# A graph layer with 40 instead of 32 hot regions: 640 hot slots and 1656 edges a later part

## The chip, the cores and the metric

The kernel runs on one core of a Trainium2 chip. Its time is the device time of one execution in microseconds (us), and less is better. A core has five engines that run their own instruction streams: PE (matmuls; PEld is its weight load), DVE, ACT, POOL and SP. Semaphores order them; DMA queues are fed by SP (plain transfers) and POOL (indirect gathers).

## The reference, cut to what matters

```python
def ref(x, src, dst, W1, b1, W2, b2, W4, b4):
    theta = x[dst] - x[src]
    w = sigmoid(relu(theta @ W1 + b1) @ W2 + b2)
    agg = segment_sum(w * theta, dst, num_segments=N)
    indeg = segment_sum(ones((E, 1)), dst, num_segments=N)
    return layernorm(x + agg + indeg * (x @ W4 + b4))
```

N = 12500 nodes of 128 values, E = 412,500 edges: 200,000 random pairs in both directions and one loop per node, sorted by dst. So the dst of consecutive edges lie close together, and their src are spread over all nodes.

## The kernel before, in words

*Edges to parts.* The edges are cut, in their sorted order, into parts. The first PLAIN = 26 parts are *early* and have 1024 edges each. After them come NF = 253 full *later* parts of CE = 1524 edges and one tail. Two parts make a block `b`, whose sums over dst cover WB = 112 nodes. `early_part(s)` and `part(s)` issue the work of step s; from the first later part on, the order in which an engine gets its instructions is the order in which the program issues them.

*Early: a table.* The first stage turns x into a table z in HBM, in twelve chunks (`table_chunk`): a row holds the node's product with W1 and the node itself. Row buffers `zbuf[4:7]` are lent to it as staging. While it runs, the early parts follow; later parts gather rows of 1 KB from z.

*Cold and hot edges.* Every edge of a later part needs two rows, that of its dst and that of its src. The dst rows come from one-hot products, since a block has few dst. Of the src rows, 1024 are *cold*: `gather(s)` brings them by eight indirect DMAs on POOL (L377) of 128 rows each, with a memset as a pause before each (L371), into one of NZ = 7 row buffers; gather(s+3) is issued in step s and waits for the last matmul of the step before (`paced`, `newest`). The rest have a src below 8192, which is in HR = 32 *hot regions* of HOT = 256 nodes, whose rows stay in SBUF (`tabs`). Each region gives a part HS = 16 slots, so a part has HK = 512 hot slots, in HQ = 4 *hot tiles* of 128.

*The hot path.* Four regions make a group; a *fetch* computes one group's hot rows for eight parts at a time. `LEADS` says how far ahead of its parts each of the eight groups is due, so that before the change there is one fetch a step. A fetch `f` goes through four functions: `hot_load` (SP, L949: the slot numbers, broadcast to all partitions), `hot_tiles` (ACT, L960 and L962: a one-hot matrix from them), `hot_products` (PE, L974: one-hot times the region's rows into the PSUM tile pd), and `hot_out` (ACT, L988: pd into xT, a ring of HX = 10 parts, in one or two writes).

*A later step.* `part(s)` runs, in this order: `hot_load` of the fetch due 7 steps later, `hot_out` of the fetch of the step before, `hot_tiles` of the one due 4 steps later (`fetch_step`), `one_hot` of a block ahead (ACT, L835 and L836), `logits` (DVE, L890, L892, L893: dst minus src rows, times w2 behind the relu, and the row sums), `gather(s+3)`, `add_part(s-1)` (PE, L1061: the weighted rows times one-hots into the PSUM tile pa), `hot_products`, `open_gate` (ACT, L897), `hot_logits` (DVE, L1032: one instruction per hot tile, from px), the sigmoid of these (ACT, L1035), `weigh` (DVE, L922: half of the cold rows), `hot_weights` (ACT, L1041: one scaling per hot tile; DVE, L1044: the one-hots owh of the hot edges), `gate_sums`, `one_hot_w` (DVE, L871: the one-hots ow of the cold edges), `weigh_rest` (ACT, L913: four scalings), and `products_ahead(s+1, s+2)` (PE: px of the next part by transposes of xT in L1013, by W1 in L1016 and the dst rows in L1020, and y of the part after it in L1024). Every second step ends a block: `total` (ACT, L1099), `finish` (DVE, L1107), `own` (ACT, L1115 and L1116), `shift`, `normalize`. Last comes `spend`, for the placement.

*Placement.* Parts are placed in sets of 64 (`place`): set 0 in the early stage, set i from part 26 + 64 i - 72 on (set 1 from the first later parts). Its edges lie as lists on 128 partitions, WL = 763 elements each. A set runs one *round* per hot region: a MAX8 (L548) finds the next eight edges of the region in each list, a MATCH_REPLACE8 (L551) takes them out, and one operation (L544) prepares the next region. Then a scan of the cold edges in NC = 5 chunks, and the results go to HBM (`hot_s`, `rows_d`). All this is a generator of steps, nearly all on DVE. `spend` lets `part(s)` run steps as long as it has *credit*: a part brings 3.0, a "k" step costs 0.85, an "s" step 3.5, an "m" step 2.5. `load(i)` (L181 and on) reads a set's edges; in the last set some of the 64 rows are missing and are filled with constants.

*The bank of constants.* The PSUM tile `fix` is one bank of 512 floats a partition: iota_f (112), own_f (128, written by `own`), w2_b (128) and gate (16). L871 and L1044 read iota_f, L892 reads w2_b, L897 writes gate and L922 reads it. px has a tile of two banks: hot_y in one, hot_x in the other, four tiles of 128 columns each, so that both are full.

*Fallback.* Every part checks that its edges found a slot and its block's dst fit the 112 nodes. If any did not, a flag sends the program to `any_dst`, which computes everything again, from the edges as they come.

## Time and profile before

| | |
|---|---|
| time, median of 3 runs | 3644.98 us (3637.49 to 3654.82) |
| the profiled execution | 3640.54 us, of which the span of its instructions 3638.8 |
| mean granted TensorE clock | 0.866 of full speed |
| gathers (L377) | 2028, 968 ns each in the mean |
| fetches' slot numbers (L949) | 226 transfers of 128 KB |

A line of the profile's table of groups gives a source line, engine and operation, output and inputs, the count, then the busy time with the mean in ns, and the idle time just before such instructions with what ended it. A row of the timeline gives the start and the duration in us, then engine, line and operation, and in brackets the wait before it with its releaser; "x4" is four like instructions in a row, with the time from the first's start to the last's end. A row of windows gives the window, its length, busy us and count for each engine asked for, then the granted clock, the share of DMA time and GB/s.

The early stage takes the first 479 us; part 26, the first later one, follows. The placements of sets 1 to 3 begin in steps 29, 85 and 149, three steps behind their loads.

### The profile page before, as it was taken

To read this page: it belongs to the slowest core of one execution; us is meant where nothing else is said; L and a number is where in the kernel's file an instruction comes from. 1 tells how busy PE (TensorE), PEld (TensorE's weight loads), DVE (VectorE), ACT (ScalarE), POOL (GpSimd) and SP (SyncE) were. 2 spreads that over 40 slices of the span, in tenths; PEclk is the share of its full clock that TensorE was granted. 3 is DMA by queue.
4 is the path that set the end of the run, shared out by engine and by line. 5 is a ranking of instruction groups with operands and counts; after the bars stand their busy time and mean duration, and the time that the engine had idled before them with its cause. 6 is when DMAs were issued, how large, how long until landed. Compare 5 with 4: busy or idle time off the path is not lost.

```text
span 3638.8 us, 60470 instructions
## 1 busy us (share of the span) xinstructions
PE 2670.6 (73%) x17515; PEld 2263.0 (62%) x17515; DVE 2627.9 (72%) x6043; ACT 2325.4 (64%) x5830; POOL 2940.3 (81%) x4273
## 2 busy tenths in 40 slices
PE   6797877766777776777676677666777777777776
PEld 5575666666666666666665566656666666666665
DVE  7365448888886789888765788989765565666556
ACT  5364667666666766666765666665766666666664
POOL 5436378888888888888888788888888888888884
PEclk9587878888889889888898788988888999899987
DMA  8333244444444444444443344444444444444442
GB/s 261 126 100 95 72 119 110 117 118 113 120 115 125 118 118 120 111 120 116 117 121 110 103 116 119 117 114 119 117 115 119 120 117 117 119 119 113 120 113 64
DMA packets 272672, 425.92 MB, mean 117 GB/s; under 512 B 67255, under 2 KB 181466, under 8 KB 272334
## 3 DMA queue, kind: packets, MB, share of 16 engines
q0 software_dynamic: 106304, 289.03, 28.7%
q1 hardware_dynamic: 164060, 126.53, 12.7%
q10 hardware_dynamic: 1970, 6.40, 0.6%
q8 instruction: 146, 2.39, 0.3%
q14 instruction: 192, 1.57, 0.1%
HBM read 393.72 MB, written 28.01 MB: 116 GB/s over the span
## 4 chain that ended last, share of the span: by engine, by line
DVE 30%; ACT 19%; PE 19%; issue 10%; POOL 9%; another core or an unknown queue 8%; DMA 2%; SPq 1%; DVEq 0%; POOLq 0%; ACTq 0%
POOL zbuf L377 6%; DVE zbuf L892 4%; DVE zbuf L890 4%; DVE lg L893 4%; PE pa L1061 4%; DVE hh L1032 3%; ACT wxh L1041 3%; ACT zbuf L913 3%; ACT of L960 3%; POOL rest_t L371 2%; PE px L1016 2%; PE px L1020 2%; PE pd L974 2%; ACT oh L835 2%
## 5 line engine op out<-in xcount | busy, mean ns | idle before, releaser
L377 POOL DMA_INDIRECT zbuf<-z,src_i x2028 | 1963.3, 968 | 454.1 <-issue 310.1
L371 POOL MEMSET rest_t<- 128x320 f32 x2028 | 774.0, 382 | 1.0
L974 PE MATMUL pd<-of,tabs 128*128 128x128 f32 (+3 forms) x4176 | 587.7, 296 | 162.3 <-ACT of L962 79.2
L974 PEld LDWEIGHTS pd<-of,tabs 128*128 128x128 f32 x4176 | 541.6, 208 | 198.7 <-issue 99.8
L1013 PE MATMUL px<-wni,xT 128*128 128x128 f32 x1016 | 207.7, 338 | 612.4 <-ACT wxh L1041 492.9
L1061 PE MATMUL pa<-zbuf,ow 128*112 128x260 f32 (+1 forms) x2444 | 627.6, 398 | 24.1 <-issue 14.8
L1013 PEld LDWEIGHTS px<-wni,xT 128*128 128x128 f32 x1016 | 133.3, 166 | 662.0 <-ACT wxh L1041 527.2
L1032 DVE SCALAR_TENSOR_TENSOR hh<-px,w_r 128x128 f32<-128x128 f32 x1016 | 294.1, 289 | 343.5 <-remote 277.6
L1061 PEld LDWEIGHTS pa<-zbuf,ow 128*112 128x112 f32 x2444 | 418.6, 192 | 160.0 <-issue 58.2
L1024 PE MATMUL y<-y,oh 64*128 64x128 f32 x2032 | 399.7, 341 | 12.2 <-issue 10.9
L1020 PE MATMUL px<-y,oh 64*128 64x128 f32 x2032 | 391.7, 340 | 12.4 <-issue 11.5
L913 ACT ACTIVATE zbuf<-zbuf 128x128 f32<-128x128 f32 x1224 | 389.0, 390 | 0.4
L988 ACT ACTIVATE xT<-pd 128x512 f32<-128x512 f32 (+7 forms) x436 | 169.8, 411 | 340.8 <-remote 181.4
L1016 PE MATMUL px<-wni,xT 128*128 128x128 f32 x2032 | 371.9, 342 | 5.4 <-issue 5.3
L1020 PEld LDWEIGHTS px<-y,oh 64*128 64x128 f32 x2032 | 324.6, 236 | 62.1 <-issue 47.1
L1016 PEld LDWEIGHTS px<-wni,xT 128*128 128x128 f32 x2032 | 343.8, 254 | 8.9 <-issue 8.8
L960 ACT ACTIVATE of<-hot_src,nodes 128x512 f32<-128x512 f16 (+2 forms) x522 | 340.5, 702 | 12.1 <-PE pd L974 7.8
L1024 PEld LDWEIGHTS y<-y,oh 64*128 64x128 f32 x2032 | 326.4, 236 | 21.1 <-issue 20.5
L892 DVE SCALAR_TENSOR_TENSOR zbuf<-zbuf,fix 128x1024 f32<-128x1024 f32 x254 | 310.1, 1221 | 17.5
L890 DVE TENSOR_TENSOR zbuf<-y,zbuf 128x1024 f32<-128x1024 f32 x254 | 309.9, 1220 | 15.2 <-PE y L1024 3.6
L893 DVE TENSOR_REDUCE lg<-zbuf 128x8 f32<-128x1024 f32 x254 | 309.8, 1220 | 8.7
L1061 PE MATMUL pa<-wxh,owh 128*112 128x130 f32 x2032 | 292.6, 279 | 21.5 <-issue 20.0
(286 smaller groups left out, 4376.1 us busy)
## 6 DMA issues: line engine op xcount, KB each, us to landing
to_all<-off_d SPq DMA_DIRECT2D x254, 128.0 KB
zbuf<-z,src_i POOLq DMA_INDIRECT x2028
hot_src<-hot_s SPq DMA_DIRECT2D x226, 128.0 KB
z<-zbuf SPq DMA_DIRECT2D x12, 1024.0 KB
xw<-in_x_dram SPq DMA_DIRECT2D x140, 56.0 KB
u<-u_d SPq DMA_DIRECT2D x140, 56.0 KB
out_dram<-o SPq DMA_DIRECT2D x140, 56.0 KB
y<-z SPq DMA_DIRECT2D x272, 28.0 KB
```

What stands on the lines that cost most here:

```text
L371: rest = nc.gpsimd.memset(rest_t, 0.0) if s >= PLAIN else nc.gpsimd.engine_nop()
L377: ins = nc.gpsimd.indirect_dma_start(out=rows_of(s)[:, k, :], out_offset=None, in_=z if s >= NH else x, in_offset=IndirectOffsetOnAxis(ap= ...
L890: nc.vector.tensor_sub(half, yy.to_broadcast([P, 2, J, D]), half)
L892: nc.vector.scalar_tensor_tensor(h, h, 0.0, w2.to_broadcast([P, K, D]), op0=OP.max, op1=OP.mult)
L893: nc.vector.tensor_reduce(lg[:, :, 0], h, AX.X, OP.add)
L913: nc.scalar.activation(wx[:, k, :D], wx[:, k, :D], AF.Copy, scale=wx[:, k, D:D + 1])
L960: nc.scalar.activation(of[:, t, :], hot_src[:, i % NU, :w], AF.Abs, bias=nodes[:, t:t + 1])
L974: newest[0] = nc.tensor.matmul(to[:, q], tabs[:, g * RG + q, t, :], of[:, t, q], start=t == 0, stop=t == HT - 1)
L1016: nc.tensor.matmul(hot_y(s, q), xT[:, q * P:(q + 1) * P], wneg, start=q == 0, stop=False, skip_group_check=True)
L1020: newest[0] = nc.tensor.matmul(hot_y(s, q), parts[s]["oh"][:, BP + q * P:BP + (q + 1) * P], y_of(s), start=False, stop=True, skip_group_ch ...
L1024: newest[0] = nc.tensor.matmul(y[:, q, :], parts[t]["oh"][:, q * P:(q + 1) * P], y_of(t), start=True, stop=True)
L1061: newest[0] = nc.tensor.matmul(to if len(w.shape) == 3 else to[:, 0, :], one, w, start=first and i == 0, stop=last and i == len(terms) - 1)
```

## The change

HR goes from 32 to 40: the hot regions now cover src below 10240, a part has 640 hot slots in five hot tiles, and CE rises from 1524 to 1656. The cold slots stay 1024, so gathers and cold work per part stay as they are. There are 233 full later parts and a tail where there were 253 and a tail, lists of 829 elements for 763, and 40 rounds for 32 in a placement; the scan has four chunks for five.

px's two banks have no room for a fifth hot tile. Its hot_y and hot_x go to `fix` (`last_y`, `last_x`); own_f moves to SBUF for it. products_ahead, hot_logits and hot_weights loop over HQ as before, now five times.

Ten fetches come in eight steps, so two of eight steps get two. `fetch_step` goes: a step builds the tiles of its first fetch as before and does its products right after `add_part`, with a lead of 3 for 4 steps; the second fetch's hot_out of the first and its own hot_tiles stand on ACT between `one_hot_w` and `weigh_rest`, its products on PE after `products_ahead`. `hot_load` is issued 5 instead of 7 steps ahead. NZ goes from 7 to 6. The table chunks take two lent row buffers and a piece of xT in place of three row buffers. The transposes of hrel in the placement go in groups of four and one.

```diff
-NZ = 7
+NZ = 6
+LEAD = 3
...
-HR = 32
+HR = 40
-LEADS = (0, 1, 2, 3, 4, 5, 6, 7)
+LEADS = (0, 1, 2, 2, 3, 4, 5, 6, 6, 7)
-CE = 1524
+CE = 1656
...
     fix = cps.tile([P, 512], F32, name="fix")
     iota_f = fix[:, :WB].rearrange("p (o m) -> p o m", o=1)
-    own_f = fix[:, WB:WB + D]
-    w2_b = fix[:, WB + D:WB + 2 * D]
+    w2_b = fix[:, WB:WB + D]
+    last_y = fix[:, 2 * P - 2 * K:3 * P - 2 * K]
+    last_x = fix[:, 3 * P - 2 * K:4 * P - 2 * K]
+    assert WB + D <= 2 * P - 2 * K and HQ == G + 1
+    own_f = const.tile([P, D], F32, name="own_f")
     gate = fix[:, 512 - 2 * K:].rearrange("p (i k) -> p i k", k=K)
     w2_f = w2_r.rearrange("p (o m) -> p o m", o=1)
...
+    stage = [t[:, :, :2 * D] for t in zbuf[NX:]]
+    stage.append(xT_flat[:, HX * HK - 2 * BE:].rearrange("p (k d) -> p k d", k=K))
+    assert late_at + 2 * NS <= HX * HK - 2 * BE
...
         hrel = pp.tile([P, S2, HQ], BF16, name="hrel")
-        pt = scratch()[:, :HQ * P].rearrange("p (q j) -> p q j", q=HQ)
-        for q in range(HQ):
...
+        for q0 in range(0, HQ, G):
+            n_q = min(G, HQ - q0)
+            pt = scratch()[:, :n_q * P].rearrange("p (q j) -> p q j", q=n_q)
...
-        NC = 5
+        NC = 4
...
-            zt = zbuf[NX + c % 3][:, :, :2 * D]
+            zt = stage[c % len(stage)]
...
         def hot_y(s, q):
-            return parts[s]["px"][:, q * P:(q + 1) * P]
+            return parts[s]["px"][:, q * P:(q + 1) * P] if q < G else last_y
 
         def hot_x(s, q):
-            return parts[s]["px"][:, P * G + q * P:P * G + (q + 1) * P]
+            return parts[s]["px"][:, P * G + q * P:P * G + (q + 1) * P] if q < G else last_x
...
                 for q in range(HQ):
-                    nc.tensor.matmul(hot_x(s, q), xT[:, q * P:(q + 1) * P], ident, start=q == 0,
+                    nc.tensor.matmul(hot_x(s, q), xT[:, q * P:(q + 1) * P], ident, start=q % G == 0,
                                      stop=False, is_transpose=True, skip_group_check=True)
                 for q in range(HQ):
-                    nc.tensor.matmul(hot_y(s, q), xT[:, q * P:(q + 1) * P], wneg, start=q == 0,
+                    nc.tensor.matmul(hot_y(s, q), xT[:, q * P:(q + 1) * P], wneg, start=q % G == 0,
                                      stop=False, skip_group_check=True)
...
-        def fetch_step(s):
-
-            for f in rest_of:
-                if f[0] - 4 == s:
-                    hot_tiles(f)
-                    tiled.append(f)
+        def due_at(s, lead):
+            return [f for f in rest_of if f[0] - lead == s]
...
-            for f in due + [f for f in rest_of if max(f[0] - 7, PLAIN - 3) == s]:
+            for f in due + [f for f in rest_of if max(f[0] - 5, PLAIN - 3) == s]:
                 hot_load(f)
...
+            now = due_at(s, 3)
+            for f in now[:-1]:
+                hot_tiles(f)
+                hot_out(f, hot_products(f))
+            for f in now[-1:]:
+                hot_tiles(f)
+                if s == PLAIN - 1:
+                    opened.append((f, hot_products(f)))
+                else:
+                    tiled.append(f)
             if s + 2 >= PLAIN:
                 one_hot(PLAIN + 2 * h)
...
             for f in rest_of:
-                if f[0] - 7 == s:
+                if f[0] - 5 == s:
                     hot_load(f)
...
             if opened:
                 hot_out(*opened.pop())
             advance("c")
-            fetch_step(s)
+            now = due_at(s, 3)
+            if now:
+                hot_tiles(now[0])
             if h == 1 and s + 3 < NS:
                 one_hot(s + 3)
             if s < NS:
                 logits(s)
-            if PLAIN + AHEAD <= s + 3 < NS:
+            if PLAIN + AHEAD <= s + LEAD < NS:
                 if s >= PLAIN + 4:
-                    paced[s + 3] = newest[0]
-                gather(s + 3)
+                    paced[s + LEAD] = newest[0]
+                gather(s + LEAD)
             if PLAIN <= s - 1 < NS:
                 add_part(s - 1)
-            if tiled:
-                f = tiled.pop()
-                opened.append((f, hot_products(f)))
+            if now:
+                opened.append((now[0], hot_products(now[0])))
             if s < NS:
                 open_gate(s)
                 hot_logits(s)
...
                 hot_weights(s)
                 gate_sums(s)
                 one_hot_w(s)
+                if now[1:]:
+                    hot_out(*opened.pop())
+                    hot_tiles(now[1])
                 weigh_rest(s)
                 products_ahead(s + 1, s + 2)
+                if now[1:]:
+                    opened.append((now[1], hot_products(now[1])))
```

More of the change, by code (lines that the diff above doesn't have):

```diff
@@ L574, in place @@
         hrel = pp.tile([P, S2, HQ], BF16, name="hrel")
-        pt = scratch()[:, :HQ * P].rearrange("p (q j) -> p q j", q=HQ)
-        for q in range(HQ):
-            nc.tensor.matmul(pt[:, q, :], hd[:, q * P:(q + 1) * P], ident_b, start=True, stop=True)
-        if i:
-            yield "c"
-        for at in (slice(h * S2, (h + 1) * S2) for h in range(LISTS)):
-            nc.scalar.activation(hrel[at].rearrange("p j q -> p q j"), pt[at, :, at], AF.Copy)
+        for q0 in range(0, HQ, G):
+            n_q = min(G, HQ - q0)
+            pt = scratch()[:, :n_q * P].rearrange("p (q j) -> p q j", q=n_q)
+            for q in range(n_q):
+                nc.tensor.matmul(pt[:, q, :], hd[:, (q0 + q) * P:(q0 + q + 1) * P], ident_b,
+                                 start=True, stop=True)
+            if i:
+                yield "c"
+            for at in (slice(h * S2, (h + 1) * S2) for h in range(LISTS)):
+                nc.scalar.activation(hrel[at, :, q0:q0 + n_q].rearrange("p j q -> p q j"), pt[at, :, at],
+                                     AF.Copy)
         hot_s = dram.tile([HR // RG, S2, LISTS, RG * HE], F16, name=f"hot_s{i}")
```

9 lines of the change are left out of this document (3 added, 6 removed).

## The prediction

> **What bounds the kernel now.** I read the page first: its span, its busy line and its forty slices.
>
> ```profile
> span 3638.8 us, 60470 instructions
> ...
> PE 2670.6 (73%) x17515; PEld 2263.0 (62%) x17515; DVE 2627.9 (72%) x6043; ACT 2325.4 (64%) x5830; POOL 2940.3 (81%) x4273
> ...
> DVE  7365448888886789888765788989765565666556
> ...
> POOL 5436378888888888888888788888888888888884
> ```
>
> POOL sits at 8 tenths from slice 7 to the last but one, whatever the others do. DVE alternates: three plateaus of 8 to 9 and stretches of 5 to 6. The plateaus are the placements of sets 1 to 3 (`place`), the rest is plain part work. So I counted parts (one L893 each) by stage; the columns are DVE time in L893 and its count, then clock, DMA share, GB/s.
>
> ```profile
> 1262.00:1580.00 318.00, 31.72 (x26) 0.87 0.42 116
> 902.00:997.00 95.00, 8.54 (x7) 0.86 0.43 119
> 997.00:1097.00 100.00, 10.98 (x9) 0.89 0.43 117
> 2700.00:3450.00 750.00, 74.42 (x61) 0.91 0.43 118
> ```
>
> A part takes 318/26 = 12.2 us during the 32 rounds of a placement, 195/16 = 12.2 in its later steps, and 750/61 = 12.3 with no placement. The same windows by engine (PE, PEld, DVE, ACT, POOL), with the early parts in the last row:
>
> ```profile
> 1262.00:1580.00 318.00, 226.10 (x1587) 199.97 (x1585) 284.72 (x598) 212.12 (x534) 280.68 (x409) 0.87 0.42 116
> 2700.00:3450.00 750.00, 572.24 (x3750) 472.86 (x3750) 455.46 (x1054) 496.70 (x1262) 653.17 (x982) 0.91 0.43 118
> 130.00:479.00 349.00, 283.33 (x1519) 217.21 (x1519) 182.29 (x431) 191.76 (x454) 162.27 (x184) 0.78 0.32 89
> ```
>
> DVE is 90% busy in the rounds (10.95 us of 12.2) and 61% outside (7.5 us of 12.3). POOL is 88 and 87%. Its eight gathers a part start 1.50 us apart, with nothing between but the pause and the issue:
>
> ```profile
> 3056.16 0.95 POOL L377 DMA_INDIRECT zbuf<-z,src_i  x1 [0.17 <-issue]
> 3057.11 0.38 POOL L371 MEMSET rest_t<- 128x320 f32 x1
> 3057.66 0.95 POOL L377 DMA_INDIRECT zbuf<-z,src_i  x1 [0.17 <-issue]
> ```
>
> 8 x 1.50 = 12.0 us. Two limits thus lie within 2% of each other: the gathers everywhere, and DVE inside the placements. Outside them DVE and ACT wait on PE instead:
>
> ```profile
> L893 DVE TENSOR_REDUCE lg<-zbuf 128x8 f32<-128x1024 f32 x61 | 74.4, 1220 | 2.1
> ...
> L1032 DVE SCALAR_TENSOR_TENSOR hh<-px,w_r 128x128 f32<-128x128 f32 x244 | 70.9, 291 | 184.5 <-remote 165.7 <-PE pa L1061 12.4
> ...
> L988 ACT ACTIVATE xT<-pd 128x512 f32<-128x512 f32 (+7 forms) x103 | 42.1, 418 | 153.6 <-remote 94.0 <-PE y L1024 50.2 <-PE px L1020 4.9
> ```
>
> This is the stage from 2700 to 3450 us. DVE stands 184.5/61 = 3.0 us a part at hh, whose input is PE's px; "remote" is a release that the trace cannot name, but L1032's only operand from another engine is px.
>
> **Part by part.** *Fewer parts.* 385,876 later edges are 253 full parts and a tail before, 233 and a tail after: 254 - 234 = 20 parts less. At 12.2 us that is **-244 us**, and 20 x 8 gathers leave POOL. Nothing on POOL grows within a part.
>
> *The fifth tile shares a bank.* hot_y and hot_x of q = 4 go to `fix`, which holds iota_f, w2_b and gate. The bank was ordered as a whole already: ow (L871) reads the columns of iota_f, and yet waited for ACT's write of own_f (L1116) into other columns.
>
> ```profile
> L871 DVE TENSOR_TENSOR ow<-fix,rel 128x448 f32<-128x448 f32 x306 | 187.4, 613 | 51.7 <-ACT fix L1116 30.6 <-PE pa L1061 12.1 <-PE pd L822 3.5
> ```
>
> The change takes own_f out, but puts a PE write, a DVE read and an ACT read in, every part. As built, four waits follow: (a) L904, the w2 multiply (L892 before), waits for PE's last matmul of products_ahead(s); (b) the fifth hh waits for ACT's gate (L909); (c) owh (L1056) waits for ACT's fifth scaling (L1053); (d) PE's fifth transpose waits for ow (L883). Before, L892 and L893 ran while PE made px, owh started beside ACT, and PE needed only ACT's scaling. The Trainium skill, page "PSUM — Partial Sum Buffer", Terms, says that two engines in one bank at the same time are a collision, reads against reads included; by it (c), a read behind a read, cannot be dropped, and the forecast below holds, while without (a) to (d) the faster rival's sum would. No run here shows such a collision.
>
> The turn that (c) breaks, in a part of the rounds:
>
> ```profile
> 1415.90 0.29 DVE L1032 SCALAR_TENSOR_TENSOR hh<-px,w_r 128x128 f32<-128x128 f32 x1
> ...
> 1416.24 0.29 DVE L1032 SCALAR_TENSOR_TENSOR hh<-px,w_r 128x128 f32<-128x128 f32 x1
> ...
> 1416.79 0.68 DVE L922 TENSOR_TENSOR zbuf<-zbuf,fix 128x512 f32<-128x512 f32 x1
> 1416.90 0.30 ACT L1035 ACTIVATE wxh<-lgh,b_c 128x4 f32<-128x4 f32 x1 [0.93 <-DVE hh L1032]
> 1417.23 1.14 ACT L1041 ACTIVATE wxh<-px,wxh 128x128 f32<-128x128 f32 x4
> 1417.38 0.62 DVE L1044 TENSOR_TENSOR owh<-fix,hrel 128x448 f32<-128x448 f32 x1
> ```
>
> ACT ends four scalings at 1418.37, a fifth at 1418.62 (they start 0.25 apart: (1.14 - 0.37)/3, one being 368 ns). owh would start at 1418.67 in place of 1417.38: **1.29 us** of idle DVE. In every second part DVE waits for ACT anyway:
>
> ```profile
> L1107 DVE TENSOR_TENSOR a<-a,pa 112x130 f32<-112x130 f32 x13 | 3.8, 291 | 20.1 <-ACT a L1099 10.8 <-ACT zbuf L913 9.3
> ```
>
> 20.1/13 = 1.55 us of wait swallow the 1.29 there, so only ACT's extra 0.25 shows. Mean (1.29 + 0.25)/2 = **0.77 us**. Lower bound 0 (ACT ahead of DVE, which its 0.93 wait speaks against), upper 1.29.
>
> *More DVE work.* A fifth hh: 1416.24 - 1415.90 = 0.34 us. owh on 560 for 448 elements: 617 x 0.25 = 0.15, of which half is covered by the wait above: 0.08. The placement steps work on 829 for 763 elements:
>
> ```profile
> L548 DVE MAX8 ed<-ew 128x8 f32<-128x763 f32 x31 | 29.6, 954 | 0.7
> L544 DVE SCALAR_TENSOR_TENSOR ew<-ew 128x763 f32<-128x763 f32 x31 | 29.5, 952 | 0.8
> L551 DVE MATCH_REPLACE8 ew<-ed,ew 128x763 f32<-128x763 f32 x30 | 29.5, 983 | 0.0
> ```
>
> 8.6% of 0.96 us is 0.083 a step, and the credit of 3.0 at 0.85 buys 3.5 steps a part: 0.29. In the rounds the part so grows by 0.77 + 0.34 + 0.08 + 0.29 = 1.5; I add 0.1 for (a), where px is now and then late for L904: **+1.6 us, 13.9 a part**. Between 0.7 (no idle at all) and 2.3 (all of 1.29, and 0.4 at L904).
>
> *More rounds.* 40 x 3 - 1 = 119 steps for 95: 119 x 0.85/3 = 34 parts for 27. The scan loses one of five chunks (3.5/3 = one part). With some 45 parts a set before (27 of rounds, 16 as counted, 2 in front), a set takes 50 after, 150 of 234 parts for three, against 135 of 254.
>
> *Outside the sets.* By (a) the 3.0 us of wait move from hh to L904, and L904 and L905 (2 x 1.25) come after px. The chain of a part is then px, L904, L905, five hh, the sigmoid, five scalings, owh, ow, px. Px alone:
>
> ```profile
> 3068.05 0.66 PE L1013 MATMUL px<-wni,xT 128*128 128x128 f32 x4 [1.73 <-issue]
> ...
> 3070.41 0.27 PE L1020 MATMUL px<-y,oh 64*128 64x128 f32 x1
> ```
>
> 2.6 us, and about as much with the fifth tile, four transposes being done ahead of (d). Sum: 2.6 + 2.5 + 1.7 + 1.75 + 1.3 and 0.25 for five hand-overs = 10.1, at half clock up to 2.6 more. That is under the gathers' 12.2 if nothing else stands in the way (the lower bound). The upper: all that is put behind px (2.5 + 0.34 + 0.25 + 0.9) comes on top of today's 12.3: 16.3. On the other side ACT's 153.6/61 = 2.5 us at hot_out go: with tiles three steps ahead in place of four, the slot of xT that hot_out overwrites was read a part earlier. PE's own matmuls rise by about a sixth (fifth tile, ten fetches for eight) on 572/750 = 76% busy. I take **12.8**, near the chain and the gathers.
>
> *Two fetches in one step,* in 2 of 8 parts: a second hot_out and tile build on ACT ahead of weigh_rest.
>
> ```profile
> L960 ACT ACTIVATE of<-hot_src,nodes 128x512 f32<-128x512 f16 x122 | 80.7, 712 | 0.0
> ...
> L962 ACT ACTIVATE of<-of 128x1024 f32<-128x1024 f32 x61 | 64.4, 1056 | 1.9
> ```
>
> 2 x 0.71 + 1.06 + 0.6 = 3.1 us on an ACT at 8.1 of 12.3 in the mean; with one-hot and five scalings some 13 in such a part, and less in the next. Queued behind it are weigh_rest, which add_part of the next step needs, and sh. At nothing inside the sets (13.9), in the 12.8 outside; without that cover 2 x 3.1/8 = 0.8 a part.
>
> *Six buffers, shorter leads.* gather(s+3) waits for products_ahead(s), which PE does after add_part(s-2), so the buffer of part s-3 is free: nothing. hot_load stands two steps ahead of its tile for three: 25 us, for an issue of 0.4 us and a 128 KB transfer: nothing, but for the next item. own_f in SBUF: nothing.
>
> *The last set's load* stops SP. Rows of set 1, then of set 3:
>
> ```profile
> 1176.61 1.12 SPq L181 DMA_DIRECT2D es<-in_src_dram  x2
> ...
> 1961.57 0.70 SPq L181 DMA_DIRECT2D es<-in_src_dram  x2
> ...
> 1968.85 9.88 SPq L181 DMA_DIRECT2D ed<-in_dst_dram  x2
> 1978.78 10.09 SPq L184 DMA_DIRECT2D ed<-in_dst_dram  x1
> ...
> 2002.84 0.82 SPq L949 DMA_DIRECT2D hot_src<-hot_s  x2
> ...
> 2010.45 1.24 ACT L835 ACTIVATE oh<-to_all,away,mine 128x1024 f32<-128x1024 bf16 x1 [30.54 <-DMA to_all<-off_d]
> ```
>
> SP is held from 1961.6 to 2002.8, 41 us, and ACT waits 30.5 for to_all behind it. Set 3 now has 41 full rows of 829 for 61 of 763: 41 x 41/61 x 1.086 = 30 us, so a stall near 18 (0 if it goes as the 64 rows of set 1; 30 if nothing changes): **-12**.
>
> *Early parts.* Set 0 gets 24 more steps of about 1 us (8 rounds) and longer ones, two more fetches ahead of the first later part, and 1 MB more of tables. DVE is 52% busy there, PE 81%: between 0 and 36 us, **+15**.
>
> *Sum.* After: 150 x 13.9 + 84 x 12.8 = 3160. Before by the same scheme: 135 x 12.3 + 119 x 12.2 = 3112. +48 - 12 + 15 = **+51 us**. The profiled execution took 3640.5 us (1.7 beside its span), 4.5 under the median of 3645.0; +51 on the median is 3696.
>
> **The rivals.** *The gathers set the pace everywhere (faster).* The waits fall into gaps: no idle at owh, px always done before L904. Then sets cost 12.3 + 0.7 = 13.0 and the rest 12.25: 150 x 13.0 + 84 x 12.25 = 2979, -133 - 12 + 15 = -130: **3515**. For it: POOL's 87% and 8 x 1.50 = 12.0, and a chain of 10.1. Against: DVE's 90% has no room for 1.5 us, and ACT waits for hh in the rounds. It decides if DVE's idle at L1056 is under 0.3 us.
>
> *PE becomes the bound.* Its sixth more of work and (d) make px late for L904 inside the sets too: 14.4 there, 14.0 outside: 2160 + 1176 = 3336, +224 - 12 + 25: **3880**. For it: the 3.0 us at hh, and 76% busy at a clock of 0.91. Against: in the rounds hh never waits for px. The Trainium skill, "TensorE: Matmul & The Clock Gate", Part 1, has the clock halve after an idle window; waits (a) and (d) would then slow px itself.
>
> *It doesn't do what it says.* A part holds 1024 + 640 = 1664 slots for 1656 edges; a flag sends the kernel to any_dst if one overflows. 403 blocks x 8 x 3 indirect transfers of 0.95 us: over 9 ms.
>
> **How the numbers follow.** Forecast 58%, its own range 3635 to 3780; gathers 25%; PE 15%; any_dst 2%. Range 3510 to 3840: about a tenth is left out on each side. Half a per cent (18 us) is about what a measurement of this kernel tells from no change. Faster: 0.24 from the gathers and 0.04 from the forecast's low end, 0.28. Same: 0.11. Slower: 0.61.
>
> **What would show it.** L1056 with some 1.3 us of idle behind ACT L1053 in every second part; L904 waiting for PE outside the sets and hh no longer; 13.9 us a part in the rounds, and 34 parts of them; POOL's share falling to near 75% with waits for PE; L1000 (hot_out) with little wait left; L847's stall of the last set near 18 us. Wrong if the rounds run at 13.0 or less, or the parts outside at 12.3.

## The result and the profile after

The changed kernel takes 3694.16 us in the median of four runs (3682.32 to 3713.01), the kernel before 3642.89 beside it: a ratio of 1.0137, 95% interval 1.0117 to 1.0157, so slower by 1.4%. The profiled execution took 3687.88 us with a span of 3686.1, 47 us more than before; forecast were 51, and the medians differ by 51.

The page of the changed kernel: the span, the busy line and two of the lines of forty slices.

```profile
span 3686.1 us, 63253 instructions
...
PE 2765.7 (75%) x18895; PEld 2404.7 (65%) x18895; DVE 2695.4 (73%) x6268; ACT 2419.8 (66%) x5936; POOL 2716.1 (74%) x3949
...
DVE  7486448888888678888787558888888766666665
...
POOL 5446367778777778787777867778877788888883
```

POOL fell from 81 to 74% of the span: its gathers became fewer and none shorter (964 ns for 968), and it no longer sits at 8 in every slice but falls to 7 in DVE's plateaus. These are longer now.

The same windows by stage as before the change, by the row sums L905 (one a part; the columns are the window, its length, DVE's busy time in that line with its count, clock, DMA share, GB/s):

```profile
570.00:1035.00 465.00, 41.48 (x34) 0.85 0.41 109
1313.00:2009.00 696.00, 61.00 (x50) 0.87 0.40 107
2904.00:3667.00 763.00, 73.28 (x61) 0.89 0.41 111
```

34 parts with rounds at 465/34 = 13.68 us, 50 parts for a whole set at 13.92, and 763/60 = 12.71 a part (from the first start to the last) after the last placement. Made from the starts of L893 and L905, part by part, the span divides so:

| stage | before | after |
|---|---|---|
| up to the first later part | 487.7 | 482.9 |
| parts 26 to 28 | 37.1 | 57.4 |
| parts with rounds, three sets | 81 at 12.19 | 102 at 13.66 |
| a whole set, 50 parts | | 13.92 a part |
| the step that waits for the last set's load | 42.7 | 30.4 |
| the other later parts | 83 at 12.4 | 67 at 14.0 |
| parts after the last placement | 85 at 12.13 | 60 at 12.71 |
| from the last row sums to the end | 18.6 | 19.2 |

Without the row of a whole set, which the others contain, each column adds up to its span within 6 us. Not only the parts with rounds grew: the 67 others, most of them in the rest of a placement, take 1.6 us longer too.

DVE's groups of a placement in the changed kernel (1363 to 1813 us, 33 parts); behind the second bar stands the idle time before them, and what ended it:

```profile
L904 DVE SCALAR_TENSOR_TENSOR zbuf<-zbuf,fix 128x1024 f32<-128x1024 f32 x33 | 40.3, 1222 | 3.8 <-issue 0.5
...
L556 DVE MAX8 ed<-ew 128x8 f32<-128x829 f32 x39 | 39.9, 1022 | 0.9
...
L1056 DVE TENSOR_TENSOR owh<-fix,hrel 128x560 f32<-128x560 f32 x33 | 24.5, 741 | 39.6 <-ACT wxh L1053 37.2 <-issue 2.4
...
L1044 DVE SCALAR_TENSOR_TENSOR hh<-fix,w_r 128x128 f32<-128x128 f32 x33 | 9.6, 291 | 5.6 <-issue 1.4 <-ACT fix L909 1.0 <-ACT of L974 0.3
...
L1119 DVE TENSOR_TENSOR a<-a,pa 112x130 f32<-112x130 f32 x17 | 4.9, 291 | 6.7 <-ACT a L1111 4.3 <-issue 1.6 <-ACT zbuf L925 0.8
```

Of the kernel before (1262 to 1580 us, 26 parts), the line of owh:

```profile
L1044 DVE TENSOR_TENSOR owh<-fix,hrel 128x448 f32<-128x448 f32 x26 | 16.0, 617 | 0.0
```

DVE waits 39.6/33 = 1.20 us at owh in each part, for ACT's fifth scaling, where it did not wait before. At the block's sum L1119 it waits 6.7/17 = 0.39 in two parts for 1.55. Both are turns that the prediction named.

Outside the placements (2914 to 3670 us) the wait stands at L904 now, as (a) has it, and ACT's wait at hot_out has shrunk from 2.5 us a part to 41.4/60 = 0.7:

```profile
L904 DVE SCALAR_TENSOR_TENSOR zbuf<-zbuf,fix 128x1024 f32<-128x1024 f32 x60 | 73.3, 1221 | 164.0 <-remote 83.5 <-PE fix L1032 75.4 <-PE pd L986 4.8
...
L902 DVE TENSOR_TENSOR zbuf<-y,zbuf 128x1024 f32<-128x1024 f32 x59 | 72.2, 1224 | 3.3 <-issue 0.8
...
L1000 ACT ACTIVATE xT<-pd 128x512 f32<-128x512 f32 (+7 forms) x117 | 43.0, 410 | 41.4 <-PE pd L986 38.6 <-remote 2.7
```

One turn of that stage, from L904 to the next L904 (timeline; start, length, engine, line, and in brackets the wait):

```profile
2953.62 1.22 DVE L904 SCALAR_TENSOR_TENSOR zbuf<-zbuf,fix 128x1024 f32<-128x1024 f32 x1 [2.09 <-PE fix L1032]
2954.88 1.22 DVE L905 TENSOR_REDUCE lg<-zbuf 128x8 f32<-128x1024 f32 x1
...
2957.74 0.30 ACT L1047 ACTIVATE wxh<-lgh,b_c 128x5 f32<-128x5 f32 x1 [1.34 <-DVE hh L1044]
2958.08 1.14 ACT L1053 ACTIVATE wxh<-px,wxh 128x128 f32<-128x128 f32 x4
2959.09 0.38 ACT L1053 ACTIVATE wxh<-fix,wxh 128x128 f32<-128x128 f32 x1
...
2959.51 0.74 DVE L1056 TENSOR_TENSOR owh<-fix,hrel 128x560 f32<-128x560 f32 x1 [1.20 <-ACT wxh L1053]
...
2960.17 0.61 DVE L883 TENSOR_TENSOR ow<-fix,rel 128x448 f32<-128x448 f32 x1
...
2960.93 0.30 PE L1025 MATMUL fix<-wni,xT 128*128 128x128 f32 x1 [1.00 <-DVE ow L883]
...
2964.55 0.63 PE L1032 MATMUL fix<-y,oh 64*128 64x128 f32 x2
...
2965.82 1.22 DVE L904 SCALAR_TENSOR_TENSOR zbuf<-zbuf,fix 128x1024 f32<-128x1024 f32 x1 [2.43 <-PE fix L1032]
```

This is a closed ring through the bank: L904, row sums, the five hh, sigmoid, scalings, owh, ow, PE's fifth transpose, px, and L904 again, 12.2 us after the first. Eight gathers need 12.0, but DVE hardly waits for their rows (3.3 us at L902 in 59 parts): here the ring sets the pace.

The load of the last set still stops ACT at to_all, for 21.2 us in place of 30.5, and the first later part has a wait of its own: its fifth hh waits 11.4 us for ACT's gate, which is queued behind the work of two fetches (the rows show the second one's).

```profile
2183.82 1.35 ACT L847 ACTIVATE oh<-to_all,away,mine 128x1152 f32<-128x1152 bf16 x1 [21.21 <-DMA to_all<-off_d]
...
495.83 1.32 ACT L972 ACTIVATE of<-hot_src,nodes 128x512 f32<-128x512 f16 x2
497.19 1.06 ACT L974 ACTIVATE of<-of 128x1024 f32<-128x1024 f32 x1
498.15 0.25 ACT L909 ACTIVATE fix<-lg,b_c 128x8 f32<-128x8 f32 x1
...
498.43 0.29 DVE L1044 SCALAR_TENSOR_TENSOR hh<-fix,w_r 128x128 f32<-128x128 f32 x1 [11.42 <-ACT fix L909]
```

### The profile page after: what moved, and what is told of

Read it like the earlier page. It is cut to its first block, busy times and chain, and to the rows that moved or that the text cites. A ratio compares the mean times of both kernels' runs of the same rounds, so it can differ in the third digit from the quotient of the medians.

```text
span 3686.1 us, 63253 instructions
## 1 busy us (share of the span) xinstructions
PE 2765.7 (75%) x18895; PEld 2404.7 (65%) x18895; DVE 2695.4 (73%) x6268; ACT 2419.8 (66%) x5936; POOL 2716.1 (74%) x3949
## 4 chain that ended last, share of the span: by engine, by line
DVE 35%; ACT 20%; PE 18%; issue 12%; POOL 5%; DMA 5%; another core or an unknown queue 4%; DVEq 1%; SPq 0%; POOLq 0%; ACTq 0%
ACT wxh L1053 7%; DVE hh L1044 6%; DVE zbuf L904 6%; DVE lg L905 6%; DVE zbuf L902 5%; POOL zbuf L385 4%; ACT zbuf L925 3%; DMA zbuf<-z,src_i 3%; PE px L1032 3%; PE px L1028 3%; PE pd L986 2%; DVE ed L556 2%; DVE ow L883 2%; PE pa L1073 2%
## 5 line engine op out<-in xcount | busy, mean ns | idle before, releaser
L385 POOL DMA_INDIRECT zbuf<-z,src_i x1866 | 1798.7, 964 | 711.2 <-issue 233.7
L379 POOL MEMSET rest_t<- 128x320 f32 x1866 | 711.8, 381 | 0.9
L986 PE MATMUL pd<-of,tabs 128*128 128x128 f32 (+4 forms) x4816 | 621.8, 284 | 51.3 <-ACT of L974 36.4
L986 PEld LDWEIGHTS pd<-of,tabs 128*128 128x128 f32 x4816 | 582.8, 198 | 73.8 <-ACT of L974 40.1
L1025 PE MATMUL px<-wni,xT 128*128 128x128 f32 x936 | 182.0, 326 | 557.1 <-ACT wxh L1053 445.7
L1073 PE MATMUL pa<-zbuf,ow 128*112 128x260 f32 (+1 forms) x2282 | 553.8, 389 | 13.9 <-ACT zbuf L925 8.5
L904 DVE SCALAR_TENSOR_TENSOR zbuf<-zbuf,fix 128x1024 f32<-128x1024 f32 x234 | 285.8, 1221 | 274.8 <-remote 118.4
L972 ACT ACTIVATE of<-hot_src,nodes 128x512 f32<-128x512 f16 (+3 forms) x602 | 395.4, 711 | 20.3 <-remote 8.3
L1056 DVE TENSOR_TENSOR owh<-fix,hrel 128x560 f32<-128x560 f32 x234 | 173.5, 741 | 281.0 <-ACT wxh L1053 229.3
L1028 PE MATMUL px<-wni,xT 128*128 128x128 f32 x1872 | 356.2, 354 | 0.0
L974 ACT ACTIVATE of<-of 128x1024 f32<-128x1024 f32 (+3 forms) x301 | 310.8, 1032 | 9.3
L909 ACT ACTIVATE fix<-lg,b_c 128x8 f32<-128x8 f32 x234 | 62.5, 267 | 373.3 <-DVE lg L905 236.3
L1073 PEld LDWEIGHTS pa<-wxh,owh 128*112 128x112 f32 x2340 | 292.8, 177 | 20.6
```

What stands on the lines that cost most here:

```text
L379: rest = nc.gpsimd.memset(rest_t, 0.0) if s >= PLAIN else nc.gpsimd.engine_nop()
L385: ins = nc.gpsimd.indirect_dma_start(out=rows_of(s)[:, k, :], out_offset=None, in_=z if s >= NH else x, in_offset=IndirectOffsetOnAxis(ap= ...
L904: nc.vector.scalar_tensor_tensor(h, h, 0.0, w2.to_broadcast([P, K, D]), op0=OP.max, op1=OP.mult)
L972: nc.scalar.activation(of[:, t, :], hot_src[:, i % NU, :w], AF.Abs, bias=nodes[:, t:t + 1])
L974: nc.scalar.activation(of, of, AF.Relu, scale=-1.0, bias=1.0)
L986: newest[0] = nc.tensor.matmul(to[:, q], tabs[:, g * RG + q, t, :], of[:, t, q], start=t == 0, stop=t == HT - 1)
```

## The experiments

They ran in three sessions. The kernel before took 3484, 3575 and 3574 us in them, the early stage and the parts outside the placements being faster than in the runs above, so every ratio is to the kernel before in its own session, and stages are compared within one where that is possible: the changed kernel did not run in the first session, and the kernel before left a profile in the second alone. The rounds do not differ: 12.19 us a part for the kernel before and 13.65 to 13.71 for the changed one in every profile.

### One wait alone, in the kernel before

The wait (c) was put into the kernel before, with four hot tiles and nothing else.

```diff
-                nc.scalar.activation(wx[:, q, :D], hot_x(s, q), AF.Copy, scale=wx[:, q, D:D + 1])
+                scaled = nc.scalar.activation(wx[:, q, :D], hot_x(s, q), AF.Copy, scale=wx[:, q, D:D + 1])
...
-            nc.vector.tensor_tensor(
+            late = nc.vector.tensor_tensor(
                 owh, iota_f.to_broadcast([P, HQ, WB]),
...
+            tc.add_manual_dep(
+                late.ins, scaled.ins.name,
+                mybir.DependencyInfo(mybir.DependencyClass.Sync, mybir.DependencyReason.DATA),
```

> The kernel before with one added wait: owh (L1044) waits for ACT's last scaling (L1041 of q = 3), as the shared bank makes it wait in the changed kernel. No fifth tile, nothing else. Theory: in the rounds owh starts 1.0 us later in each part (end of four scalings at 1418.4 against 1417.4 in the turn shown), half of it is swallowed where DVE waits for ACT anyway (L1107, 1.55 us in two parts): rounds from 12.2 to 12.7, some 135 parts in and around the placements, +50 to +70 us, ratio 1.014 to 1.020; outside the placements nothing. Rival, DVE has the slack (the gathers set the pace, DVE was only put at 90%): less than +20 us, ratio below 1.006.

3633.65 us, ratio 1.0162 (1.0137 to 1.0187): 58 us more. Rounds at 12.68 us for 12.19, the 85 last parts at 11.80 for 11.82 in the kernel before of that session. DVE's groups of 1262 to 1580 us:

```profile
L1044 DVE TENSOR_TENSOR owh<-fix,hrel 128x448 f32<-128x448 f32 x25 | 15.6, 624 | 23.6 <-ACT wxh L1041 19.8 <-issue 3.8
...
L1111 DVE TENSOR_TENSOR a<-a,pa 112x130 f32<-112x130 f32 x12 | 3.5, 291 | 6.2 <-ACT a L1103 4.1 <-ACT zbuf L913 2.1
```

0.94 us of wait at owh in each part, and 6.2/12 = 0.52 in two parts at the block's sum, where the kernel before has 1.55: half was swallowed. The theory holds in place and size; DVE has no slack in the rounds.

> The kernel before, for its profile on this chip. Theory: rounds at 12.2 us a part as on the other chip (DVE and gathers), early stage near 415 us, the 30 us stall at the last set's load still there, outside the placements 11.8 to 12.0: 3484. Rival: a chip with a faster part everywhere (rounds below 12).

3581.39 us, span 3579.5; rounds at 12.19, 85 last parts at 11.82, but the early stage takes 481.0 us, not 415: the second session of runs is not as fast as the first. The stall before set 3 is there (19 parts of 242 us).

### The wait at owh made shorter, then taken away

Two edits to the changed kernel. In the first, ow fills the time in which owh waits:

```diff
                 weigh(s)
+                one_hot_w(s)
                 hot_weights(s)
                 gate_sums(s)
-                one_hot_w(s)
```

> The changed kernel, but one_hot_w(s) (ow, 0.61 us on DVE) stands ahead of the five scalings and of owh. Theory: in the rounds DVE stands idle at owh (1.20 us a part) only because owh shares a bank with ACT's fifth scaling; ow fills 0.6 us of it, and up to 0.3 a part comes back at the sum of two parts (L1119, now 0.39 us in two parts). Rounds fall from 13.66 to 13.1 to 13.35 us, outside nothing changes: over 150 parts 45 to 85 us less, 3610 to 3650. Rival, another wait takes the place (hh on ACT's gate, L1119): rounds at 13.6, less than 15 us.

3459.09 us, ratio 0.9943 (0.9923 to 0.9964), rounds at 13.38, just above the expected range. In the second, both one-hots read the constants from SBUF (iota_row), so (c) and (d) go:

```diff
+    iota_s = iota_row[:, :WB].rearrange("p (o m) -> p o m", o=1)
...
-                    ow, iota_f.to_broadcast([P, J, WB]),
+                    ow, iota_s.to_broadcast([P, J, WB]),
...
-                owh, iota_f.to_broadcast([P, HQ, WB]),
+                owh, iota_s.to_broadcast([P, HQ, WB]),
```

> The changed kernel, but ow and owh read the constants 0 to 111 from SBUF in place of the bank that holds the fifth tile: waits (c) and (d) go, (a) and (b) stay. Theory: the wait of 1.20 us a part at owh goes, about half of it comes back at L1119 (1.55 us in two parts before the change), rounds fall from 13.66 to about 13.0 us, outside nothing: 150 x 0.65 = 95 less, about 3600. Rival: two operands in SBUF are slower for DVE (owh above 0.74 us, ow above 0.61), or disturb POOL, and eat the gain: 3660 or more.

3409.84 us, ratio 0.9775 (0.9747 to 0.9802), rounds at 13.01: with two edited lines the kernel is 2.3% faster than the one before. DVE in 34 parts of the rounds (owh and the block's sum), the reordered kernel:

```profile
L1056 DVE TENSOR_TENSOR owh<-fix,hrel 128x560 f32<-128x560 f32 x34 | 25.2, 742 | 22.7 <-ACT wxh L1053 22.7
...
L1119 DVE TENSOR_TENSOR a<-a,pa 112x130 f32<-112x130 f32 x17 | 5.0, 292 | 15.8 <-ACT a L1111 15.8
```

and the one that reads SBUF:

```profile
L1057 DVE TENSOR_TENSOR owh<-iota_row,hrel 128x560 f32<-128x560 f32 x34 | 25.4, 747 | 0.0
...
L1120 DVE TENSOR_TENSOR a<-a,pa 112x130 f32<-112x130 f32 x17 | 5.0, 292 | 28.5 <-ACT a L1112 28.5
```

What goes at owh comes back in part at the block's sum, which waits for ACT. In the rounds the expected 13.0 was met. The expected totals were reckoned from the runs of the first section, and the changed kernel did not run in that session, so the totals are read against the kernel before alone.

### The multiply by w2

```diff
-            w2 = w2_b.rearrange("p (o d) -> p o d", o=1)
+            w2 = w2_r.rearrange("p (o d) -> p o d", o=1)
```

> The changed kernel, but L904 reads w2 from SBUF, so wait (a) for PE's last matmul of products_ahead goes. Theory: outside the gathers set the pace and L904's 2.7 us of wait only move to hh, as before the change; in the rounds L904 waits 0.1 us: 0 to 15 us less, 3680 to 3694. Rival, (a) lengthens the chain that sets the pace outside: 12.7 falls to 12.2 there, 40 us or more, 3655 or less. Third: SBUF operands make L904 slower than 1.22 us, 3700 or more.

3537.49 us, ratio 1.0159 (1.0142 to 1.0176). Rounds at 13.65, as without the edit; the 60 last parts at 12.28. L904 itself takes 1226 ns for 1221 and never waits, yet POOL's gathers are longer. POOL in the last parts, the kernel with the edit, then, from the same session, the one with ow first:

```profile
L385 POOL DMA_INDIRECT zbuf<-z,src_i x452 | 465.3, 1029 | 78.9 <-issue 63.9 <-ACT zbuf L925 5.7 <-ACT sh L1068 2.2
```

```profile
L385 POOL DMA_INDIRECT zbuf<-z,src_i x450 | 428.7, 953 | 78.5 <-issue 58.6 <-ACT zbuf L919 4.0 <-ACT zbuf L925 3.0
```

8 x 0.076 = 0.6 us a part more for the gathers, about the 0.55 between 12.28 and the 11.73 of the other kernel. DVE's wait has moved to the rows that the gathers bring (2785 to 3510 us):

```profile
L902 DVE TENSOR_TENSOR zbuf<-y,zbuf 128x1024 f32<-128x1024 f32 x59 | 72.3, 1225 | 137.6 <-DMA zbuf<-z,src_i 137.2
```

The gathers set the pace there, so what (a) alone costs where the ring sets it stays open.

### The gathers' wait

In the steps with two fetches `newest[0]`, which gather(s+3) waits for, is the second fetch's last matmul (L986) and not that of products_ahead. The prediction had overlooked this.

```diff
                 products_ahead(s + 1, s + 2)
+                ahead[0] = newest[0]
...
-                    paced[s + LEAD] = newest[0]
+                    paced[s + LEAD] = ahead[0]
```

> The changed kernel, but gather(s+3) waits for the last matmul of products_ahead (L1036) of the step before; in the two steps of eight with two fetches the changed kernel lets it wait for the second fetch's products (L986), which PE does behind that. Theory: outside the placements the gathers set the pace (8 x 1.50 = 12.0 us) and stop for that wait, so the 60 parts after the last placement fall from 12.7 to 12.2 or 12.3 us each, POOL's idle time behind L986 (28 us there) goes, the rounds stay at 13.66, and some 80 parts save 35 to 40 us: about 3656. Rival, the chain px, L904, hh, scalings, owh, ow sets the pace outside: the parts stay at 12.7, about 3694.

3518.04 us, ratio 1.0098 (1.0081 to 1.0114); the last 60 parts at 11.79, below what was expected. But the kernel with ow first reached 11.73 in that session without this edit. So both kernels were run side by side.

> The changed kernel unchanged, beside its variants: the first four experiments ran on a chip on which the kernel before takes 3484 us, not 3643, and whose early stage is some 70 us shorter. Theory: the rounds are a matter of DVE and take 13.66 us a part here too; the 57.4 us of the first three later parts and the 12.7 us outside the placements hung on PE at a lower granted clock, and are near 40 and 11.8 us here, so that moving the gathers' wait (first experiment) gains nothing here: ratio to before 1.010 to 1.013, and 13.9 us a part over the 50 parts of a set. Rival: the gathers' wait for the second fetch costs here as well; then the ratio is 1.02 or more and the 60 last parts take 12.3 or more.

3653.59 us, ratio 1.0205 (1.0179 to 1.023), last 60 parts at 12.43. These are the rival's numbers, and the theory's 11.8 outside was not met. But the kernel before took 3575 us here and not 3484, so this tells nothing of the first session.

> The changed kernel once more, as the measure for the run with the moved wait, since the two earlier sessions differ (3484 and 3575 us for the kernel before). Both theories: ratio to before 1.012 to 1.023, rounds 13.65 us a part.

3660.67 us, ratio 1.0235 (1.0212 to 1.0258), just above the expected 1.023; last 60 parts at 12.47.

> The first experiment (gathers wait for products_ahead, not for the second fetch) beside the changed kernel on one chip. Theory: where the changed kernel takes 12.4 us or more in the 60 last parts, POOL stops for L986 in the steps with two fetches, and without that wait they take 12.0 to 12.1: 25 to 35 us less over some 80 parts; where it takes 11.9 or less there, nothing. Rival: in the fourth variant of the second session the shorter turn on DVE (ow, owh) did it, and the moved wait alone leaves the parts where they are.

3653.89 us, ratio 1.0226 (1.0208 to 1.0243): 7 us, within the intervals. The last 60 parts take 12.29. POOL in them, the changed kernel and then the one with the moved wait:

```profile
L385 POOL DMA_INDIRECT zbuf<-z,src_i x457 | 435.7, 953 | 102.5 <-issue 62.5 <-PE pd L986 20.1 <-ACT zbuf L925 5.0
```

```profile
L385 POOL DMA_INDIRECT zbuf<-z,src_i x457 | 435.5, 953 | 91.5 <-issue 60.5 <-PE fix L1033 12.1 <-remote 5.0
```

The theory that this wait makes the parts outside slow falls: 20.1 us of wait for L986 go and 12.1 for the end of px (L1033 there) take their place. In that session DVE waits at L904, behind px, and for rows only 3.2 us in 60 parts, so the ring sets the pace. In the first session, with the clock at 0.93 in this stage in place of 0.91, the same kernel waited at L902 for the gathers' DMA instead. DVE in the last parts of the two, third session and then first:

```profile
L904 DVE SCALAR_TENSOR_TENSOR zbuf<-zbuf,fix 128x1024 f32<-128x1024 f32 x60 | 73.3, 1221 | 134.4 <-PE fix L1033 77.5 <-remote 43.6 <-PE pd L987 5.4
```

```profile
L902 DVE TENSOR_TENSOR zbuf<-y,zbuf 128x1024 f32<-128x1024 f32 x59 | 72.3, 1225 | 73.8 <-DMA zbuf<-z,src_i 72.9
```

### The last set's load

The load of the rows of a set with missing parts was cut into powers of two, here in the kernel before (61 rows into 32, 16, 8, 4 and 1):

```diff
+                r = 0
+                while r < full:
+                    c = 1 << ((full - r).bit_length() - 1)
-                nc.sync.dma_start(t[h * S2:h * S2 + full, :m], bass.AP(
-                    tensor=edges.tensor, offset=edges.offset + e0 + h * HL, ap=[[CE, full], [1, m]]))
+                    nc.sync.dma_start(t[h * S2 + r:h * S2 + r + c, :m], bass.AP(
+                        tensor=edges.tensor, offset=edges.offset + e0 + r * CE + h * HL, ap=[[CE, c], [1, m]]))
+                    r += c
```

> The kernel before, with the last set's load cut into transfers of 32, 16, 8, 4 and 1 rows in place of 61. Theory: SP's 41 us over rows that go one after the other are the cause of the 30 us stall before set 3, so it goes with them and nothing else moves: 25 to 30 us less, ratio 0.992 to 0.993. Rival: the stall belongs to the tail row or to the first-dst transfers; then it stays, ratio above 0.997.

3559.25 us, ratio 0.9958 (0.9938 to 0.9977). SP's queue in it, and ACT's wait at to_all:

```profile
1927.58 3.66 SPq L184 DMA_DIRECT2D es<-in_src_dram  x10
...
1931.63 3.77 SPq L184 DMA_DIRECT2D ed<-in_dst_dram  x10
1935.45 0.25 SPq L188 DMA_DIRECT2D ed<-in_dst_dram  x1
...
1948.28 1.24 ACT L839 ACTIVATE oh<-to_all,away,mine 128x1024 f32<-128x1024 bf16 x1 [4.92 <-DMA to_all<-off_d]
```

SP is held for some 11 us in place of 41, ACT's wait falls from 30.5 to 4.9 (36.6 in the second session), and parts 130 to 148 take 215 us for the 242 of the second session. So in its place the edit saves the expected 27; the whole run gained only 15, short of the expected 25 to 30. The 85 last parts took 8 us more in this profile than in that of the second session; the rest of the difference isn't explained.

### Together, and the block's sum moved

The eighth run puts ow first, lets owh alone read SBUF, moves the gathers' wait and cuts the load.

> The changed kernel with four edits: ow stands ahead of the scalings and reads the bank; owh alone reads the constants from SBUF; the gathers' wait is for products_ahead, as in the first experiment; the last set's load is cut into transfers of 32, 8 and 1 rows. Theory: no idle time at owh, rounds at 12.9 to 13.0 (the second experiment had 13.38 with 0.6 of idle left), the gather hardly longer (953 ns, against 983 with both one-hots from SBUF), the step with the last set's load near 14 us in place of 30: 3370 to 3400, ratio 0.967 to 0.976. Rivals: the gathers are as slow as in the third experiment and outside 0.2 a part is lost (3400 to 3420); the rows' transfers hold SP as long in pieces (15 more).

3510.58 us, ratio 0.9809 (0.9789 to 0.9829), outside the expected 0.967 to 0.976: that was reckoned from the first session. Rounds 13.06, a little above the expected 12.9 to 13.0; the step with the last set's load 12.1 us, 31.0 in the changed kernel of that session; last 60 parts 12.07. No wait is left at owh, but the block's sum has all of it, 28.8/17 = 1.7 in two parts:

```profile
L1125 DVE TENSOR_TENSOR a<-a,pa 112x130 f32<-112x130 f32 x17 | 5.0, 291 | 28.8 <-ACT a L1117 20.3 <-ACT zbuf L930 8.5
```

That wait hangs on the order on ACT, so total was moved ahead of the cold scalings:

```diff
                 hot_weights(s)
+                if h == 0 and ended:
+                    total(b - 1)
                 gate_sums(s)
...
             if h == 0 and ended:
-                total(b - 1)
+                if s >= NS:
+                    total(b - 1)
                 finish(b - 1)
```

> The eighth run's kernel (ow ahead of the scalings, owh from SBUF, the gathers' wait moved, the last set's load cut up), with total(b-1) (L1117 there, 0.26 us on ACT) moved ahead of gate_sums and weigh_rest. Theory: what was taken from the wait at owh came back at the block's sum (1.7 us in every two parts, behind ACT's four scalings of cold rows and total). With total ahead of these, 1.5 of it goes: rounds from 13.05 to 12.3, 0.6 to 0.75 a part over 150 parts, 90 to 110 us less than the eighth run; ratio to before 0.950 to 0.957. Rival, the gathers (12.0 us a part) or px now hold the rounds: above 12.7, 50 us or less.

3413.71 us, ratio 0.9562 (0.953 to 0.9594), where the changed kernel has 1.0235 in the same session, and within the expected 0.950 to 0.957. Rounds at 12.36, last 60 parts at 11.92, and at the block's sum:

```profile
L1125 DVE TENSOR_TENSOR a<-a,pa 112x130 f32<-112x130 f32 x17 | 5.0, 291 | 3.3 <-ACT a L1117 2.7 <-issue 0.4 <-ACT wxh L1059 0.2
```

This kernel beats both: 4.4% under the one before.

## Why the prediction was right, point by point

*The waits on DVE in the rounds.* The table sums DVE's wait at owh and half of that at the block's sum (which comes once in two parts), in us a part:

| kernel | at owh | half at the sum | both | a part in the rounds |
|---|---|---|---|---|
| before | 0 | 0.77 | 0.77 | 12.19 |
| before, one wait added | 0.94 | 0.26 | 1.20 | 12.68 |
| changed | 1.20 | 0.20 | 1.40 | 13.66 |
| ow first | 0.67 | 0.46 | 1.13 | 13.38 |
| one-hots from SBUF | 0 | 0.84 | 0.84 | 13.01 |
| eighth run | 0 | 0.85 | 0.85 | 13.06 |
| total early | 0 | 0.10 | 0.10 | 12.36 |

Within the kernels of five tiles a part grows by what the waits grow, 1.30 from the last row to the changed kernel. DVE thus sets the rounds, and (c) costs 1.40 - 0.77 = 0.63 us a part net, forecast 0.77. The forecast had the wait at owh in every second part; it comes in each, and the wait at the block's sum shrinks by 1.16, so that the net is near. The rest of the 1.47 us: the fifth hh with its read of the sum 0.37, and 0.17 of idle time before it, of which wait (b) for the gate is a small part (1.0 us of 5.6 in 33 parts), against 0.34 in all; owh 0.12, forecast 0.15 of which half counts; the three wide placement operations 1.18 x 3086 ns less 1.19 x 2889 = 0.20, forecast 0.29; L904's 0.05, forecast 0.1. That is 1.54, and L557, one of the short ones, takes 0.07 less (226 ns for 284). The forecast of 13.9 a part met 13.92 over the 50 parts of a set, 34 of them with rounds, both numbers as forecast. In part this is luck: 13.9 was worked out for the parts with rounds, which take 13.66, and the 14 parts behind them, which were not worked out, take 14.4 (12.6 before). DVE waits 1.20 us a part at owh there too (15.6 us in 13 parts from 1815 to 2007 us); the rest of their 1.8 was not taken apart.

*Fewer parts, longer sets.* 234 parts for 254 and three times 50 parts in placements: as built. The gain of 244 us was more than given back: 102 parts x 1.47 = 150 with rounds, some 67 x 1.6 = 107 in the other parts around them, 60 x 0.58 = 35 after the last placement, 292 together.

*Outside.* 12.71 in the last 60 parts where 12.8 was taken, but a term behind it was mis-sized. The ring was put at 10.1 us with 2.6 for px; it takes 12.2. Up to the end of ow it is about as put: 7.2 us (2953.62 to 2960.78) for 7.5 with the hand-overs. From there to L904 (2965.82) go 5.0. The 2.6 was the time from px's first recorded matmul to its last in the kernel before, those of y in between included, with the clock at 1.00 (a row of the timeline, then one of windows):

```profile
3070.41 0.27 PE L1024 MATMUL y<-y,oh 64*128 64x128 f32 x1
```

```profile
3068.00:3070.70 2.70, 2.65 (x29) 2.42 (x29) 2.60 (x8) 2.07 (x8) 2.40 (x4) 1.00 0.32 97
```

A lower clock, for which the forecast kept up to 2.6 us, does not make the difference. In the turn shown it is 0.60 while PE makes px; in the next turn it is 1.00, px's matmuls are recorded within 2.7 us of the fifth transpose, and L904 still starts 5.1 us behind ow:

```profile
2960.90:2965.20 4.30, 4.27 (x30) 3.85 (x30) 2.39 (x6) 3.42 (x7) 3.80 (x6) 0.60 0.42 103
...
2973.00:2976.00 3.00, 2.87 (x30) 2.66 (x31) 1.51 (x2) 2.61 (x7) 2.67 (x5) 1.00 0.33 93
```

```profile
2972.37 0.61 DVE L883 TENSOR_TENSOR ow<-fix,rel 128x448 f32<-128x448 f32 x1
...
2975.47 0.38 PE L1032 MATMUL fix<-y,oh 64*128 64x128 f32 x2
...
2978.05 1.22 DVE L904 SCALAR_TENSOR_TENSOR zbuf<-zbuf,fix 128x1024 f32<-128x1024 f32 x1 [3.07 <-remote]
```

In the 44 turns of this stage that take less than 13 us, those 5.0 are 5.07 in the mean. So the step that failed is px at 2.6, a row of recorded matmuls taken for the time until DVE is let go; what fills the rest is not shown. That the reserve for the clock made up for it is luck. Beyond that comes about 0.4 a part in the mean from the steps with two fetches (one part in four takes 13.8 in the mean and the others 12.35), which the forecast put at nothing. The moved wait brought 0.18 of it; the rest was not taken apart. In the eighth run and the one with total early, whose ring is shorter, the parts take 12.1 and 11.9. DVE still waits behind px there (140.6 and 175.5 us in 59 and 60 parts) and for rows only 3.2 and 11.4 us, though POOL is idle for little but its issue: ring and gathers lie close together.

*The last set's load.* The step fell from 42.7 to 30.4 us, 12 as forecast, and ACT's wait is 21.2 where near 18 was forecast; SP is held some 23 us for a forecast 30. That the rows' number in one transfer is the cause is shown by the cut loads. The Trainium skill, "DMA: Bandwidth & Descriptors", section "Why a DMA increments its semaphore by 16 and not by 1", has a transfer use the largest number of engines up to 16 that divides the rows; 61 and 41 are primes and leave one. The traces agree as far as they go: 9.88 us of SP for two loads of 61 rows, 3.77 for the ten pieces; how many engines carried them they don't tell.

*Early parts.* Forecast +15 and measured -4.8 + 20.3 = +15.5, but not for the reason given: in this pair of profiles the 24 added placement steps cost nothing, DVE being 60% busy there (130 to 479 us), and the loss is in parts 26 to 28. The hit is luck: in the later sessions the first later part starts at 479.5 to 488.7 us in the kernels with 40 regions and at 476.5 to 481.1 in those with 32, and parts 26 to 28 take 47.1 to 50.8 for 31.7 to 35.4, together some 20 us. ACT has the work of two fetches ahead of the first gate; no run moved them, so this cause is read from the trace alone.

*The rivals.* The gathers did not set the pace in the rounds: owh's wait is four times the 0.3 us from which that rival was to decide. PE did not become the bound there either: L904 waits 3.8 us in 33 parts. The fallback did not run: L385 has 1866 gathers of later parts, 233 x 8 and two for the tail. Six row buffers in place of seven cost nothing that shows: DVE waits for rows 2.0 us in 33 parts with rounds and 3.3 in 59 of the last.

*Open.* In the later sessions the change costs 2.1 and 2.35% (78 and 87 us), beside the prediction 1.4%; that the forecast met 51 us to one is luck. In the second session's profiles the kernel before is 59 us shorter than beside the prediction and the changed one 27, of which 26 and 17 in the last parts and next to nothing in the rounds. In the last parts the two are held by different things: there the kernel before now waits for rows, at 11.82 us a part, where it had waited for px, while the changed one waits behind px as it did. DVE in those parts of the second session, the kernel before (2853 to 3560 us), then the changed one (2904 to 3638):

```profile
L890 DVE TENSOR_TENSOR zbuf<-y,zbuf 128x1024 f32<-128x1024 f32 x59 | 72.2, 1224 | 198.0 <-DMA zbuf<-z,src_i 177.9 <-PE pa L1061 20.0
```

```profile
L904 DVE SCALAR_TENSOR_TENSOR zbuf<-zbuf,fix 128x1024 f32<-128x1024 f32 x60 | 73.3, 1221 | 147.6 <-PE fix L1032 70.6 <-remote 61.2 <-issue 9.6
```

Why PE's part is shorter in one session than in another was not found.

## What to carry to other kernels

A free corner of a bank isn't free: whoever moves in is ordered against all who read or write the rest of the bank, and in the rounds the price was the wait of DVE, the engine without slack. Put constants that are read in every turn where no other engine writes or reads per turn, or reorder so that other work fills the wait, and then look where the wait went: here half came back at the next hand-over, and only moving that too gave the whole gain. Fewer parts pay only as far as a part keeps its time: 20 parts fewer were worth 244 us, and the same edit lengthened the turns that set the pace in all stages, with and without rounds.

## What the runs showed of the hardware

The edits that moved an operand of the one-hots or of the multiply by w2 from the bank to SBUF made POOL's gathers longer; how, no run shows. A gather of the later parts takes 970 ns in the mean with both one-hots from the bank (first and second run), 989 with both from SBUF, and 1035 with L904's 1.2 us from SBUF, all in one session, while the DVE operations themselves keep their time (owh 747 ns for 742, L904 1226 for 1221). In the last one the last 60 parts took 0.32 to 0.55 us more than in the other three kernels of that session. With owh alone from SBUF (eighth run, total early) a gather of the last parts takes 970 and 971 ns, for 953 in the changed kernel of the same sessions. The change itself moved own_f, some 0.3 us of DVE a part, and there the gathers of the last parts stay at 952.
